# A drain of GpSimd's queue behind the gather of the last slot's rows, in a fused Mamba block and mixture of experts

## The chip, the cores and the metric

The kernel runs on one core of a Trainium2 chip. The time is the device time of one execution, in microseconds (us); of several runs the median is given. A profiled execution also has a span, from its first to its last instruction, and every time inside it is counted from the span's start. Engines: TensorE (PE, with its weight loads apart as PEld), VectorE (DVE), ScalarE (ACT), GpSimd (POOL) and SyncE (SP), which here issues the plain DMAs. A "q" behind a name (POOLq) is the engine's sequencer, which takes the program's instructions in order and runs the ones that need no datapath itself.

## What is computed

Two residual sublayers on x of 8 x 512 tokens with 256 features, each under an adaptive layer norm whose shifts, scales and gates come from a small projection of `c`. The first sublayer is a Mamba-like block (projection, causal convolution, a linear scan, a gate). The second, where the change lies, is a mixture of 8 experts with hidden size 1024, and each token goes to one expert:

```python
logits = x @ wr + br
probs = jax.nn.softmax(logits, axis=-1)
top_p, top_i = jax.lax.top_k(probs, 2)
gate = top_p[:, 0] / (top_p[:, 0] + top_p[:, 1])
top1 = top_i[:, 0]
out = jnp.zeros_like(x)
for e in range(n_experts):
    hmid = jax.nn.gelu(x @ w1[e] + b1[e], approximate=False)
    hout = hmid @ w2[e] + b2[e]
    mask = top1 == e
    out = out + jnp.where(mask[:, None], hout * gate[:, None], 0.0)
```

The reference runs every expert on every token. The kernel runs each expert only on the tokens that chose it.

## The kernel before

*Two stages.* The first runs the Mamba block over the 8 batches, writes each token's row (features, statistics, gate and the modulation vectors, 1028 floats) to the scratch `xp_d` in DRAM, and lists the tokens of each expert in `ids_d`, by 32 indirect DMAs of GpSimd (line 937). The second works through "slots". A pair slot is 256 tokens of one expert (two tiles of 128), a single slot 128.

*A slot's work.* `name_tokens` (line 1023) loads the slot's token numbers, on SP. `fetched` (1150) calls `expert_of` (1035), which loads the expert's weights and biases on SP, and `rows_of` (1055), which gathers the token rows into a tile `xg` by one indirect DMA of GpSimd for each tile of 128. `made` (1283) modulates and transposes them, `layer1` (1083) multiplies by w1 and applies Gelu, and `layer2` (1259) multiplies by w2 into the PSUM tile `py`, finishes the rows on VectorE in the tile `ot`, and scatters them to the output, again by one indirect DMA of GpSimd for each tile. `ot` has two buffers and so has `py`.

*The loop.* `work` (1289) runs over the slots with three slots fetched ahead. There are 20 slots that always run: 16 pairs and 4 singles, so 36 tiles, 36 gathers and 36 scatters. The last slot is a pair; it is fetched in the pass n = 16. Behind the loop stand two branches (`tc.If`, line 1323) for up to three more single slots, which depend on how the tokens fell; with these inputs neither is taken. In a branch's place GpSimd's sequencer then runs an INC_SWDGE_SEM[...]. After that the program closes (line 1379): among others a DRAIN on each engine, and barriers between them.

*What sets the order.* Instructions of the loop are not emitted as written. They are recorded in a `Plan`, with a length each from a table in the code, a due time, and the tiles that they read and write. `order` (191) then simulates all queues greedily: of the instructions whose inputs and buffers are there, the one that can start first goes first, and at equal starts the one that is due first. An indirect DMA is held for 1.3 on GpSimd's queue and lands 9.0 later; what waits for a DMA starts 2.2 after it has landed (`reach`, 277). `plan.call` (121) records any function as an instruction, with a queue, the tiles it reads and writes, and a length. The result is the program order of each engine; on the chip the waits are semaphores.

Of the kernel before, what the change touches and what calls it, by code (L numbers as in the profile page):

```python
# [289 lines left out]
def adaln_mamba_moe_kernel(  # L290
# [15 lines left out]
    nc = tc.nc  # L306
# [29 lines left out]
    plan = Plan(tc)  # L336
    chip, nc = nc, plan
# [93 lines left out]
    with tc.tile_pool(name="wa", bufs=1) as wa, tc.tile_pool(  # L431
# [591 lines left out]
        def name_tokens(i):  # L1023
            jb, at_ = tiles(i), where[i][1]

            def fn():
                o = chip.sync.value_load(at_, min_val=0, max_val=E * TOK)  # L1027
                chip.sync.dma_start(  # L1028
                    out=ids[:, i, 0:jb],
                    in_=ids_d[bass.ds(o, jb * P), :].rearrange("(p j) o -> p (j o)", j=jb),  # L1030
                )

            loads(fn, [ids[:, i, 0:jb]], [at_, *id_views[: FEW * NT]], 0.8)

        def expert_of(i, w1t, w2t, b1t, b2t, behind=()):

            number = where[i][0]

            def fn():
                e = chip.sync.value_load(number, min_val=0, max_val=E - 1)  # L1040
                chip.sync.dma_start(  # L1041
                    out=w1t, in_=w1[bass.ds(e, 1)].rearrange("o (k p) f -> p (o k) f", p=P)
                )
                chip.sync.dma_start(out=b1t, in_=par[:, bass.ds(e * KF, KF)])
                chip.sync.dma_start(
                    out=b2t, in_=b2[bass.ds(e, 1)].rearrange("o d -> (o d)").partition_broadcast(P)
                )
                chip.sync.dma_start(
                    out=w2t, in_=w2[bass.ds(e, 1)].rearrange("o (k p) d -> p (o k) d", p=P)
                )  # L1050

            loads(fn, [w1t, b1t, b2t, w2t], [number, *behind], 2.5)
            return i, w1t, b1t, b2t, w2t

        def rows_of(i, xg, upto):

            for j in range(tiles(i)):
                nc.gpsimd.indirect_dma_start(
                    out=xg[:, j, :], out_offset=None, in_=xp_d[0:upto, :],
                    in_offset=bass.IndirectOffsetOnAxis(ap=ids[:, i, j : j + 1], axis=0),  # L1060
                    bounds_check=upto - 1, oob_is_err=False,
                )
            return xg
# [19 lines left out]
        def layer1(t, hT, gl, ph_tile):  # L1083
            i, w1t, b1t, b2t, w2t, xg = t
            n = tiles(i) * P
            for f in range(KF):
                ph = ph_tile()
                for k in range(KD):
                    nc.tensor.matmul(
                        ph[:, 0:n], lhsT=w1t[:, k, f * P : (f + 1) * P], rhs=hT[:, k, 0:n],  # L1090
                        start=(k == 0), stop=(k == KD - 1),
                    )
                nc.scalar.activation(gl[:, f, 0:n], ph[:, 0:n], AF.Gelu, bias=b1t[:, f : f + 1])
            return gl
# [43 lines left out]
    with tc.tile_pool(name="g", bufs=2) as gp, tc.tile_pool(  # L1138
# [6 lines left out]
        plan = nc = Plan(tc, plan)  # L1145
# [4 lines left out]
        def fetched(i, xg=None):  # L1150
            t = expert_of(
                i, wts.tile([P, KD, FF], FP, name="w1t"), wts.tile([P, KF, D], FP, name="w2t"),
                blk.tile([P, KF], FP, name="b1t"), blk.tile([P, D], FP, name="b2t"),
            )
            if xg is None:

                at = next(turn) % 5
                pool, n = (blk, 3) if at < 3 else (blk2, 2)
                xg = rows_of(
                    i, pool.tile([P, JB, ROW], FP, name="xg", tag=f"xg_{n}", bufs=n),  # L1160
                    FEW * L if i < NEARLY else TOK + BLK,
                )
            return (*t, xg)

        got = [slot0, fetched(1, pre[1])] + [fetched(i) for i in range(2, NEARLY)]
# [90 lines left out]
        slots = list(range(NEARLY)) + [NEARLY + i for i in order]  # L1256
        assert sorted(slots + rest) == list(range(NEARLY + NSLOT))

        def layer2(t, gl):

            i, w1t, b1t, b2t, w2t, xg = t
            mg = xg[:, :, OWN:ROW]
            ot = gp.tile([P, JB, D], FP, name="ot")
            for j in range(tiles(i)):
                py = ps_y.tile([P, D], FP, name="py")
                for f in range(KF):
                    nc.tensor.matmul(
                        py, lhsT=gl[:, f, j * P : (j + 1) * P], rhs=w2t[:, f, :],
                        start=(f == 0), stop=(f == KF - 1),
                    )  # L1270
                nc.vector.tensor_tensor(ot[:, j, :], py, b2t, ALU.add)
                nc.vector.tensor_tensor(ot[:, j, :], ot[:, j, :], mg[:, j, 2 * D : 3 * D], ALU.mult)
                nc.vector.scalar_tensor_tensor(
                    ot[:, j, :], ot[:, j, :], xg[:, j, D + 2 : D + 3], xg[:, j, 0:D],
                    ALU.mult, ALU.add,
                )
                nc.gpsimd.indirect_dma_start(
                    out=outf[i * JB + j],
                    out_offset=bass.IndirectOffsetOnAxis(ap=ids[:, i, j : j + 1], axis=0),
                    in_=ot[:, j, :], in_offset=None, bounds_check=TOK - 1, oob_is_err=False,  # L1280
                )

        def made(t):
            return features(
                t[0], t[-1], gp.tile([P, JB, D], FP, name="hg"),
                gp.tile([P, KD, BLK], FP, name="hT"), ps_r.tile([P, KD, BLK], FP, name="tp"),
            )

        def work(slots, got, begun=None):


            ahead, pending = len(got), None
            hT = None if begun else made(got[0])
            for n in range(len(slots)):
                nc.due = behind + (n + 1) * SLOT
                if n + ahead + 1 < len(slots):
                    name_tokens(slots[n + ahead + 1])
                if n + ahead < len(slots):
                    got.append(fetched(slots[n + ahead]))
                if n == 0 and begun:  # L1300
                    nxt = begun[2]
                else:
                    nxt = made(got[n + 1]) if n + 1 < len(slots) else None
                if n == 0 and begun:
                    layer2(*begun[:2])
                else:
                    gl = layer1(
                        got[n], hT, gp.tile([P, KF, BLK], FP, name="gl"),
                        lambda: ps_h.tile([P, BLK], FP, name="ph"),
                    )  # L1310
                    if pending is not None:
                        layer2(*pending)
                    pending = (got[n], gl)
                hT = nxt
            layer2(*pending)

        name_tokens(slots[NEARLY])
        work(slots, got, (slot0, gl0, hTs[1]))
        plan.emit()
        nc = chip  # L1320
        more = nc.values_load(filled[0:1, 0:1], min_val=0, max_val=NSING)
        for at, part in ((FIRST, rest[:1]), (FIRST + 1, rest[1:])):
            with tc.If(more > at):
                for i in part:
                    name_tokens(i)
                work(part, [fetched(i) for i in part])
# [56 lines left out]
```

## Time and profile before

| | before |
|---|---|
| median of 3 runs | 602.8 us (600.97 to 606.39) |
| the profiled execution | 602.82 us |
| its span | 601.0 us |
| mean granted TensorE clock | 0.968 |
| busy: PE / DVE / ACT / POOL | 563.9 / 351.4 / 210.5 / 209.3 us |
| indirect DMAs of GpSimd: lists / gathers / scatters | 32 / 36 / 36 |
| first start of a gather / last end of a scatter's issue | 284.1 / 589.86 us |

A group's line on the page has the source line, the engine and the operation, what is written and read, and the count; behind the bar the busy time and the mean length of one in ns; behind the second bar the idle time of the engine just before, and what ended most of it. All operations that the plan records have line 154 or 159, since it issues them, so groups are told apart by their tiles. For an indirect DMA the time shown is[...] not that of the transfer. Instructions of a sequencer do not count as busy: they are found by asking for a line's instructions.

### The profile page before, as it was taken

How to read it: one execution, taken by the hardware profiler on the slowest of the kernel's cores; microseconds unless marked ns; L12 is line 12 of the kernel's file. 1: busy time of each engine (PE TensorE's matmuls, PEld its weight loads, DVE VectorE, ACT ScalarE, POOL GpSimd, SP SyncE). 2: the span in 40 equal slices, each digit the busy share in tenths (PEclk: the TensorE clock that was granted, in tenths of full speed). 3: DMA queues.
4: the chain of work that ended last, by engine and by line, in shares of the span. 5: the costliest groups of instructions: out<-in, count | busy, mean ns of one | idle time of the engine just before them, and what ended most of it. 6: DMA issues, size and time to landing. Idle time of an engine off the chain costs nothing. (4 is left out here: it accounts for less than half of the span.)

```text
span 601.0 us, 8691 instructions
## 1 busy us (share of the span) xinstructions
PE 563.9 (94%) x2882; PEld 430.1 (72%) x2882; DVE 351.4 (58%) x1087; ACT 210.5 (35%) x404; POOL 209.3 (35%) x334
## 2 busy tenths in 40 slices
PE   5999999999999999999999938999999999999990
PEld 2454766677675766767678826889888988988980
DVE  4879978987878786784876516325234343532210
ACT  2328544544553634432512210223221422222320
POOL 1513663736254453530424142233223322231110
PEclk9779999999999999999999977999999999999996
DMA  7359999410200001010829996999977977972000
GB/s 276 119 148 196 273 254 238 63 51 14 85 1 18 20 1 37 0 37 1 256 72 254 171 342 225 298 382 331 332 245 237 299 252 244 305 245 71 26 3 16
DMA packets 58703, 96.73 MB, mean 161 GB/s; under 512 B 9852, under 2 KB 41854, under 8 KB 58656
## 3 DMA queue, kind: packets, MB, share of 16 engines
q1 hardware_dynamic: 50720, 72.98, 41.2%
q0 software_dynamic: 7936, 23.17, 11.4%
q8 instruction: 24, 0.39, 0.3%
q14 instruction: 23, 0.19, 0.2%
HBM read 86.42 MB, written 22.81 MB: 182 GB/s over the span
## 5 line engine op out<-in xcount | busy, mean ns | idle before, releaser
L159 ACT ACTIVATE gl<-ph,b1t 128x256 f32<-128x256 f32 (+1 forms) x152 | 68.5, 452 | 186.8 <-PE ph L154 180.7
L154 PE MATMUL py<-w2t,gl 128*128 128x256 f32 x476 | 109.8, 383 | 0.0
L154 PEld LDWEIGHTS py<-w2t,gl 128*128 128x128 f32 x476 | 91.7, 193 | 12.9
L159 POOL DMA_INDIRECT out<-ot,ids x36 | 37.7, 1047 | 159.7 <-DVE ot L159 148.6
L159 DVE SCALAR_TENSOR_TENSOR sv<-u,pt,sv 128x512 f32<-128x512 f32 x96 | 77.2, 809 | 12.7 <-ACT sv L159 12.4
L159 PE MATMUL ph<-hT,w1t 128*128 128x256 f32 (+1 forms) x304 | 84.3, 359 | 0.0
L154 PE MATMUL ph<-hT,w1t 128*128 128x256 f32 (+1 forms) x304 | 84.2, 359 | 0.0
L159 DVE TENSOR_TENSOR ot<-py,b2t 128x256 f32<-128x256 f32 x34 | 14.4, 425 | 109.3 <-PE py L154 105.4
L159 PE MATMUL px<-xnT,wi 128*128 128x512 f32 x128 | 69.6, 626 | 0.0
L154 PE MATMUL px<-xnT,wi 128*128 128x512 f32 x128 | 65.9, 597 | 0.0
L154 PEld LDWEIGHTS ph<-hT,w1t 128*128 128x128 f32 x304 | 55.6, 191 | 6.3
L159 PEld LDWEIGHTS ph<-hT,w1t 128*128 128x128 f32 x304 | 55.0, 191 | 6.2 <-issue 0.4
L159 POOL DMA_INDIRECT xg<-xp_d,ids x36 | 37.8, 1051 | 60.9 <-DMA ids<-ids_d 40.5
L159 POOL DMA_INDIRECT ids_d<-tok,row x32 | 34.8, 1087 | 36.1 <-DVE row L159 13.7
L154 PEld LDWEIGHTS px<-xnT,wi 128*128 128x128 f32 x128 | 24.6, 192 | 31.2 <-issue 31.2
L159 ACT COPY u<-px 128x512 f32<-128x512 f32 x32 | 18.7, 585 | 62.6 <-PE px L154 62.1
L159 DVE COPY hT<-tp 128x512 f32<-128x512 f32 (+1 forms) x20 | 12.7, 634 | 36.3 <-PE tp L154 28.1
L159 PEld LDWEIGHTS px<-xnT,wi 128*128 128x128 f32 x128 | 21.3, 192 | 16.4 <-issue 14.8
L159 POOL TENSOR_TENSOR rs<-ve,nhalf 128x4 f32<-128x4 f32 x16 | 19.5, 1219 | 38.7 <-DVE ve L159 29.0
L159 ACT ACTIVATE tz<-px 128x512 f32<-128x512 f32 x32 | 19.1, 595 | 39.3 <-PE px L154 35.7
L159 DVE TENSOR_TENSOR hg<-hg,xg 128x256 f32<-128x256 f32 x72 | 28.9, 422 | 1.2
L159 DVE TENSOR_TENSOR xr<-po,h 128x256 f32<-128x256 f32 x32 | 13.5, 421 | 25.6 <-PE po L154 25.3
(347 smaller groups left out, 947.2 us busy)
## 6 DMA issues: line engine op xcount, KB each, us to landing
w1t<-in_w SPq DMA_DIRECT2D x19, 1024.0 KB
w2t<-in_w SPq DMA_DIRECT2D x19, 1024.0 KB
xp_d<-modb_d SPq DMA_DIRECT2D x8, 1536.0 KB
xp_d<-xr SPq DMA_DIRECT2D x8, 520.0 KB
xt<-in_x SPq DMA_DIRECT2D x8, 512.0 KB
bc<-mod_d SPq DMA_DIRECT2D x7, 384.0 KB
b2t<-in_b SPq DMA_DIRECT2D x19, 128.0 KB
w<-in_w SPq DMA_DIRECT2D x2, 1024.0 KB
```

The costliest lines, as they stand in the source:

```text
L154: me["calls"].append(lambda: getattr(getattr(self.nc, name), op)(*args, **kw))
L159: calls=[lambda: getattr(getattr(self.nc, name), op)(*args, **kw)],
```

## The change

In `work`, behind the fetch of the last slot, the plan gets one more instruction on GpSimd's queue: `drain()`, which has no operand. For the planner it reads the last slot's tile `xg`, writes nothing, and takes 8.0. It is recorded only while the plan is built, not in the branches behind the loop.

```diff
                 if n + ahead < len(slots):
                     got.append(fetched(slots[n + ahead]))
+                    if nc is plan and n + ahead == len(slots) - 1:
+
+                        plan.call("gpsimd", chip.gpsimd.drain, [], [got[-1][-1]], 8.0)
                 if n == 0 and begun:
                     nxt = begun[2]
```

## The prediction

> **What bounds the kernel now.** I read the page first, then the chain of waits, then the instructions that belong to the program's closing lines, then a table of stretches over the last 16 us, and last GpSimd's instructions in order of time around the place of the edit. The page:
>
> ```profile
> span 601.0 us, 8691 instructions
> ...
> PE   5999999999999999999999938999999999999990
> ...
> L159 POOL DMA_INDIRECT out<-ot,ids x36 | 37.7, 1047 | 159.7 <-DVE ot L159 148.6
> ...
> L159 POOL DMA_INDIRECT xg<-xp_d,ids x36 | 37.8, 1051 | 60.9 <-DMA ids<-ids_d 40.5
> L159 POOL DMA_INDIRECT ids_d<-tok,row x32 | 34.8, 1087 | 36.1 <-DVE row L159 13.7
> ```
>
> TensorE is busy in every slice but the last, so up to about 587 us the time is TensorE's, and GpSimd's waits there (159.7 us before the scatters) cost nothing. GpSimd issues 36 + 36 + 32 = 104 indirect transfers. The last slice of row PE is 0: the end belongs to something else. The chain of waits does not help there: it stops at 589.86 us, with the last scatter, and puts 47.48 us down to a transfer issued at 540.43, which is only the semaphore that a later instruction tested last. What fills the end is seen at line 1379, where the program closes, at line 1323 (the two branches that are not taken) and, for comparison, at line 1371, where it opens. The columns are count, then ns min/median/max, then first and last start in us:
>
> ```profile
> L1379 POOLq DRAIN  x3: 40/107/8560, 591.6 to 600.7; - x3
> L1379 SPq DRAIN  x3: 7/7/7, 592.2 to 600.4; - x3
> L1379 ACTq DRAIN  x2: 8/8/8, 577.6 to 600.4; - x2
> ```
>
> ```profile
> L1323 POOLq INC_SWDGE_SEM  x2: 2242/2244/2245, 585.8 to 589.3; - x2
> ```
>
> ```profile
> L1371 POOLq INC_SWDGE_SEM  x1: 31/31/31, 0.2 to 0.2; - x1
> ...
> L1371 POOLq DRAIN  x1: 179/179/179, 0.4 to 0.4; - x1
> ```
>
> The first of GpSimd's three closing drains, at 591.57, takes 8.56 us; the two behind it 0.107 and 0.040, the one at the start 0.179. Is it a wait for data? The stretches say no (the last two columns are the share of the DMA engines and GB/s):
>
> ```profile
> core 0: us, PE busy (x) PEld busy (x) DVE busy (x) ACT busy (x) POOL busy (x), PEclk, DMA share, GB/s
> ...
> 588.00:590.00 2.00, 0.00 (x0) 0.00 (x0) 0.21 (x1) 0.00 (x0) 0.98 (x1) 0.99 0.05 12
> 590.00:591.00 1.00, 0.00 (x0) 0.00 (x0) 0.00 (x0) 0.00 (x0) 0.00 (x0) 0.50 0.32 111
> 591.00:600.20 9.20, 0.00 (x0) 0.00 (x0) 0.00 (x0) 0.00 (x0) 0.00 (x0) 0.50 0.00 0
> ```
>
> The last scatter's packets move before 591.0; after that no engine computes and no DMA engine moves a byte for 9.2 us. So the drain is work of GpSimd's own that is left from before. A drain with nothing issued before it costs 0.04 to 0.18 us; this one has 104 transfers behind it: (8.56 - 0.11) / 104 = 0.081 us each, if it is a price per transfer. That is my reading, and the forecast hangs on it.
>
> **The change.** It adds one instruction, moves one scatter behind it in GpSimd's order, and removes nothing.
>
> *Where it goes.* The planner holds the drain back until the last slot's rows are there. In the planner's own clock, used here for the order alone, the second gather of the last slot starts at 542.20, so the drain may start at 542.20 + 1.3 + 9.0 + 2.2 = 554.70; GpSimd is free from 552.11; the second scatter of the slot then being finished is ready at 554.73. The drain goes first, by 0.03. GpSimd's stretch in the trace:
>
> ```profile
> 527.30 1.05 POOL L159 DMA_INDIRECT xg<-xp_d,ids  x1 [0.30 <-issue]
> 528.65 1.02 POOL L159 DMA_INDIRECT xg<-xp_d,ids  x1 [0.31 <-issue]
> 536.78 1.03 POOL L159 DMA_INDIRECT out<-ot,ids  x1 [7.10 <-DVE ot L159]
> 540.43 1.01 POOL L159 DMA_INDIRECT out<-ot,ids  x1 [2.62 <-DVE ot L159]
> 551.45 0.98 POOL L159 DMA_INDIRECT out<-ot,ids  x1 [10.01 <-DVE ot L159]
> 554.91 0.98 POOL L159 DMA_INDIRECT out<-ot,ids  x1 [2.48 <-DVE ot L159]
> ```
>
> So it stands between the scatters of 536.78 and 540.43.
>
> *What it costs there.* It starts at 537.81. Of 36 scatters 28 lie before it, so it deals with 32 + 36 + 28 = 96 transfers: 0.11 + 96 x 0.081 = 7.9 us, to 545.7. Queued behind it on GpSimd are the scatter of 540.43 (it goes to about 545.9, 5.5 us late) and the one of 551.45, which finds GpSimd free from 547 and is on time. Who waits for the late scatter? Only the reuse of its `ot` buffer, one of two:
>
> ```profile
> 562.52 0.42 DVE L159 TENSOR_TENSOR ot<-py,b2t 128x256 f32<-128x256 f32 x1 [2.76 <-PE py L154]
> ```
>
> A scatter's packets ended 2.1 us (the one of 536.78) to 3.4 us (540.43) after its start; from 545.9 that is 549.3, 13 us before the write. The last rows' gathers stand ahead of the drain, and SP's queue is not touched. On the planner's clock the late scatter frees its buffer at 575.2 and the first write comes at 578.08, so no other engine's order moves. Cost on the path: 0. Without that cover it would be the 7.9 us in full.
>
> *What it saves.* At the closing drain 8 transfers are left: 0.11 + 8 x 0.081 = 0.76 us in place of 8.56, a gain of 7.8. The closing drain cannot end before the last scatter has landed, though: its packets end at 590.88, and SyncE finds its semaphore set at 591.63.
>
> *The two semaphore increments at line 1323.* They run on GpSimd's sequencer, 2.24 us each. The first ends at 588.01 and the last scatter follows at 588.88, 0.67 after its data (588.21), where the scatters before it follow 0.28 after theirs: 0.39 lost. The second ends at 591.54, and only then does the drain begin. With nothing outstanding the same instruction took 0.031 (line 1371); with 103 and 104 transfers behind it 2.242 and 2.245. So after the change each costs between 0.03 and 2.245. With 7 or 8 outstanding the nearer row is that of none, so I take 0.2. Then the last scatter starts at 588.49, its packets end 2.0 later at 590.5, and it has landed by about 590.9 (between 590.5 and 591.2, from the 0.75 above); the drain ends at 591.0, and the tail of 0.84 (600.13 to 600.97) follows: span 591.9, gain 9.1. With the increments unchanged: 591.57 + 0.76 + 0.84 = 593.2, gain 7.8.
>
> **Two rules of the Trainium skill against it.** The trace has drains of 7 to 17 ns at the close on SyncE, ScalarE, VectorE and TensorE. "VectorE: DVE Perf Modes", section "The DRAIN you can't avoid", calls such drains boilerplate of about 12 ns on all five engines, the same for every kernel; by that there is nothing to win, and the time stays at 602.8. The four engines agree; GpSimd's 8,560 ns does not, and the row decides. "PSUM — Partial Sum Buffer", section "Engine vs sequencer instructions", says that a drain waits until its engine is fully idle. If that were all, the new drain would end at 537.9 and take nothing off the closing one, which would then be a cost that any first late drain pays. But GpSimd's last instruction ended at 589.86, 1.7 us before the closing drain began: idleness alone does not explain 8.56 us. The rule leaves open a price per transfer or a fixed one. No run here shows which.
>
> **The rivals.**
>
> *The price is fixed.* GpSimd's closing drain costs 8.5 us whenever any indirect transfer has gone before it since the last drain, or the new drain deals with none of it. For: only one such drain is in the trace. Against: 0.107 and 0.040 follow at once, so the work can be used up. Then 602.8, because the new drain is covered.
>
> *The price per transfer holds, the increments stay at 2.24.* For: 2.242 and 2.245 differ by less than one part in 104. Against: 0.031 at the start. Then 593.2 + 1.8 = 595.0.
>
> *Slower: the drain holds the scatter too long.* If it takes D us, the late scatter lands at 537.81 + D + 0.2 + 3.4, and the write of 562.52 starts to wait from D = 21. TensorE has the second of two `py` buffers and a layer 1 to do, up to 576.2, so the end moves by D - 34. With the gain of 7.8 it is slower from D = 42, or 0.44 us a transfer, five times the 0.081. At 0.55 a transfer (D = 53) it ends near 613. For it: the drain now runs while the weights' loads keep the DMA engines busy, which the closing one did not. Against: the factor.
>
> **How the numbers follow.** The profiled execution took 602.82 us, 1.8 over its span of 601.0, and is level with the median of the runs, 602.8. Both readings gain: increments shrinking, 591.9 + 1.8 = 593.7, chance 0.48; increments unchanged, 595.0, chance 0.31. Fixed price or no effect, 602.8: 0.14. Slower: 0.07. The likeliest is 593.7. The range runs from 591.8 (the landing at its early end and 1.5 us of scatter between runs, which went from 600.97 to 606.39) to 597.5 (595.0 with the same and a little over), which holds the first two cases, about 0.78, and leaves out the rest. About 1% (6 us) is what can be told from no change here: under 596.8 is faster. From the cases, faster 0.77, same 0.16, slower 0.07.
>
> **What would show it.** Right: a drain of 7 to 9 us on GpSimd from about 538, the scatter behind it near 546, no new wait before the write of 562.5, a first closing drain of 2 us or less, and increments far under 2.24. Wrong: a first closing drain that is still 8 us (fixed price), a new drain of a few tenths of a us (it does nothing), or a write of `ot` that waits for its scatter (held too long).

## The result, and the profile after

| | before | after |
|---|---|---|
| median | 602.7 us (4 runs, 600.97 to 606.39) | 595.14 us (4 runs, 591.9 to 595.28) |
| profiled execution / span | 602.82 / 601.0 us | 595.11 / 593.2 us |
| last scatter but one starts / span ends | 585.04 / 601.0 us | 585.90 / 593.2 us |
| from that start to the end ("the tail") | 15.96 us | 7.30 us |

The ratio is 0.9869, with a 95% interval of 0.983 to 0.9908: 1.3% faster, and at the weak end of the interval 0.9%. Ratios here and below are formed over the runs in the chip's faster state alone, while medians are of all runs, so a ratio is not exactly the quotient of the medians shown. The page of the changed kernel:

```profile
span 593.2 us, 8692 instructions
...
PE   5999999999999999999999875999999999999996
```

The last slice of row PE is 6 where it was 0: the empty end is nearly gone. GpSimd around the new drain, in order of time (start, length, then in brackets the idle time before and what ended it):

```profile
537.64 1.03 POOL L159 DMA_INDIRECT out<-ot,ids  x1 [7.11 <-DVE ot L159]
547.48 1.01 POOL L159 DMA_INDIRECT out<-ot,ids  x1 [8.81 <-issue]
552.32 0.98 POOL L159 DMA_INDIRECT out<-ot,ids  x1 [3.82 <-DVE ot L159]
555.77 0.98 POOL L159 DMA_INDIRECT out<-ot,ids  x1 [2.48 <-DVE ot L159]
```

The second scatter waits 8.81 us for nothing but its turn ("issue"), and the third waits for its data again, so the delay has died out there. The drain itself is an instruction of the sequencer and is found at its own line:

```profile
L286 POOLq DRAIN  x1: 9183/9183/9183, 537.4 to 537.4; - x1
```

Its record begins at 537.41, although in the program it stands behind the scatter of 537.64: the sequencer's record starts before GpSimd is done with what stands ahead (by 2.75 us behind two gathers in a run below). From the end of the scatter's issue (538.67) to the drain's end (537.41 + 9.18 = 546.59) are 7.92 us. That stretch, from the end of the issue ahead to the end of the drain, is what "the drain took" means from here on. The first write of the reused buffer `ot` still waits for its matmul and not for the late scatter:

```profile
563.38 0.42 DVE L159 TENSOR_TENSOR ot<-py,b2t 128x256 f32<-128x256 f32 x1 [2.76 <-PE py L154]
```

At the close (three lines further down in this kernel), count, ns min/median/max, first and last start:

```profile
L1382 SPq EVENT_SEMAPHORE  x14: 17/28/1588, 590.0 to 593.2; - x14
...
L1382 POOLq DRAIN  x3: 46/113/1997, 590.1 to 593.0; - x3
L1382 SPq DRAIN  x3: 7/7/7, 592.4 to 592.7; - x3
```

```profile
L1326 POOLq INC_SWDGE_SEM  x2: 325/325/325, 586.6 to 589.8; - x2
```

The first closing drain fell from 8.56 to 2.00 us, each increment from 2.24 to 0.325. The stretches show what the first closing drain now does:

```profile
core 0: us, PE busy (x) PEld busy (x) DVE busy (x) ACT busy (x) POOL busy (x), PEclk, DMA share, GB/s
...
590.00:591.00 1.00, 0.00 (x0) 0.00 (x0) 0.00 (x0) 0.00 (x0) 0.33 (x1) 0.57 0.16 57
591.00:593.20 2.20, 0.00 (x0) 0.00 (x0) 0.00 (x0) 0.00 (x0) 0.00 (x0) 0.50 0.08 28
```

Before, 9.2 us went by with a DMA share of 0.00. Now the last scatter's packets end at 591.36, within the drain's time (590.12 to 592.12). The price of its 8 transfers alone would have ended it at 590.88: it has become a wait for the landing.

*Which wait ends last at the close.* SyncE runs a row of EVENT_SEMAPHORE instructions, which test one semaphore after the other. The longest of its 14, the 1.588 us from 590.18 to 591.76, ends 0.40 us after the last scatter's packets and is the wait for them. Nine more tests follow about 0.06 us apart, then two drains, the last at 592.41; GpSimd goes on at 592.44, though its own drain ended at 592.12. So GpSimd's drain has 0.3 us to spare, and SyncE's row is what ends last. Before, the same row ran from 591.63 to 592.31 and was covered by the long drain. The runs below agree: where the closing drain is longer (3.33 and 2.67 us) GpSimd goes on 0.04 us after it, and where it is shorter (1.85 to 2.29 us) GpSimd goes on 0.03 us after the second of those SyncE drains.

*An offset that is not the change's.* In the profiled execution everything from about 400 us on runs 0.87 us later than before, up to the tail. The offset arises between 314 and 375 us, where the first stage gives way to the second, and ahead of the new drain. In other executions it is larger and goes both ways (in the experiments below -5.1 to +3.3 us against the kernel before), so spans of single executions are not compared with each other. The tail is: 15.96 - 7.30 = 8.66 us of gain, and 8.66 - 0.87 = 7.8 us is what is left in the span (601.0 - 593.2).

### The profile page after: what moved, and what is told of

It is laid out like the page before. It is cut to its first block, busy times and chain, and to the rows that moved or that the text cites. A ratio compares the mean times of both kernels' runs of the same rounds, so it can differ in the third digit from the quotient of the medians.

```text
span 593.2 us, 8692 instructions
## 1 busy us (share of the span) xinstructions
PE 564.6 (95%) x2882; PEld 430.7 (73%) x2882; DVE 351.0 (59%) x1087; ACT 210.7 (36%) x404; POOL 209.4 (35%) x334
## 3 DMA queue, kind: packets, MB, share of 16 engines
q0 software_dynamic: 7936, 23.17, 11.5%
## 5 line engine op out<-in xcount | busy, mean ns | idle before, releaser
L154 PEld LDWEIGHTS ph<-hT,w1t 128*128 128x128 f32 x304 | 55.6, 191 | 6.3
```

The lines of the kernel that those rows point to most:

```text
L154: me["calls"].append(lambda: getattr(getattr(self.nc, name), op)(*args, **kw))
```

## The experiments

The theory: the drain's time is work for each transfer that GpSimd has issued since its last drain (called its walk below); a transfer is paid for once, at the end or earlier; the increments shrink with it; and in the middle the drain is covered by other work. The rivals: a fixed price, a cover that fails, and no effect of the drain itself. Below, "left" is the number of transfers left for the closing drain, and an offset is how much later than in the kernel before the scatters of a run's second stage start where no drain delays them (with a minus, earlier). Each edit is shown against the kernel that the text ahead of it names; "..." marks lines left out.

**Earlier, so that more is left.** The changed kernel, with the drain behind the tenth slot's fetch instead of the last one's.

```diff
-                    if nc is plan and n + ahead == len(slots) - 1:
+                    if nc is plan and n + ahead == 9:
 
-                        plan.call("gpsimd", chip.gpsimd.drain, [], [got[-1][-1]], 8.0)
+                        plan.call("gpsimd", chip.gpsimd.drain, [], [got[-1][-1]], 5.0)
```

> The drain stands behind the gathers of the tenth slot instead of the last, and nowhere else (planned length 5.0). 61 or 62 indirect transfers lie before it, 42 or 43 behind it. Price per transfer (0.082 us each, and 0.02 us each for a semaphore increment): the new drain lasts about 5.1 us, the first closing drain 0.11 + 42 x 0.082 = 3.6 us, each increment at the branches about 1.0 us, span about 594.7. Fixed price (a drain costs 8 us whatever the number): new drain 8 us, closing drain 2.0 us as in the changed kernel, increments 0.33 us, span about 593.2.

It took 591.27 us (span 589.4), but its offset is -4.65 us. GpSimd's increments and closing drains:

```profile
L1326 POOLq INC_SWDGE_SEM  x2: 962/964/965, 581.1 to 584.2; - x2
```

```profile
L1382 POOLq DRAIN  x3: 46/107/3325, 585.2 to 589.1; - x3
```

With 40 left the closing drain takes 3.325 us, as a price per transfer has it: 0.11 + 40 x 0.0813 = 3.36. A fixed price would leave 8.5 or 2. The tail is 9.0 us. The miss: the new drain itself, with 64 transfers, took 8.5 us in place of 5.3 (taken up at the end of this section).

**Both drains.** The changed kernel, with the drain of the last experiment added.

```diff
                         plan.call("gpsimd", chip.gpsimd.drain, [], [got[-1][-1]], 8.0)
+                    if nc is plan and n + ahead == 9:
+
+                        plan.call("gpsimd", chip.gpsimd.drain, [], [got[-1][-1]], 5.0)
```

> The changed kernel with a second drain behind the gathers of the tenth slot. Price per transfer, each transfer paid once: the early drain about 5.1 us, the later one only for the 34 or 35 transfers between them, 2.9 us instead of 7.9; closing drain 2.0 us, span as the changed kernel (593.2) within 0.5. Fixed price, or a price for all transfers since the start: the later drain again 7.9 us or more.

594.94 us, span 593.1.

```profile
L286 POOLq DRAIN  x2: 4052/7272/10493, 418.7 to 537.2; - x2
```

The later drain now took 2.79 us (538.44 to 541.22) where the change's took 7.92; it has 32 transfers to deal with, and 0.11 + 32 x 0.0813 = 2.71. So what the early one had dealt with was gone: each transfer is paid once. Increments (0.322, 0.325), closing drain (2.06) and tail (7.43) are those of the change. The early one took 8.5 us again.

**More transfers, without rows.** The kernel before, with 24 small plain transfers of GpSimd (16 rows of 4 bytes) that nothing reads, and no drain.

```diff
+        tiny = tab.tile([P, 24], FP, name="tiny")
...
+                    if nc is plan and 4 <= n + ahead < 16:
+                        for k in range(2 * (n + ahead) - 8, 2 * (n + ahead) - 6):
+                            plan.ops[-1]["calls"].append(lambda k=k: chip.gpsimd.dma_start(
+                                out=tiny[0:16, k : k + 1], in_=par[0:16, k : k + 1]
+                            ))
```

> The kernel before, without a drain, and with 24 small direct transfers added to GpSimd's queue (16 rows of 4 bytes each, two behind the gathers of each of 12 slots; what they load is not used). Price per transfer: first closing drain 0.11 + 128 x 0.0813 = 10.5 us, increments 2.7 to 2.8 us. Price per row moved (104 transfers of 128 rows, so the 24 add 3 in 100): closing drain 8.8 us, increments 2.3 us. Fixed price: 8.56 and 2.24 us.

605.38 us, span 603.6, tail 18.9 us. The increments, and then the closing drains:

```profile
L1329 POOLq INC_SWDGE_SEM  x2: 2722/2728/2733, 585.7 to 589.5; - x2
```

```profile
L1385 POOLq DRAIN  x3: 46/103/10523, 592.2 to 603.3; - x3
```

10.523 us against 10.5 expected for 128 transfers: (10.523 - 8.560) / 24 = 0.082 us for each added one. By rows it would have been 8.8. By DMA packets, of which the small transfers have 32 each and the others 76 on average (8704 in all against 7936), it would have been 9.4. The span is about that of before, so the price does not go by time either. It goes by the transfer, whatever its size, and whether it is indirect or not.

**The cover taken away.** The kernel before, with a drain directly ahead of the last scatter.

```diff
+                if nc is plan and i == slots[-1] and j == JB - 1:
+                    plan.ops[-1]["calls"].insert(0, chip.gpsimd.drain)
```

> The kernel before with the drain put directly ahead of the last scatter, where no other engine has work left. If the gain is only that the drain's time is hidden: the new drain lasts about 8.5 us, the last scatter starts about 8 us later, the closing drain shrinks to 2.0 us, and the span stays within 1 us of 601.0. If a drain in the program is cheaper than one at the close: the new drain is well under 8 us and the span nears 593.

598.72 us, span 596.9, with an offset of -3.61 us. Tail: 581.43 to 596.9 = 15.5 us, against 15.96 with no drain added.

```profile
581.43 0.98 POOL L159 DMA_INDIRECT out<-ot,ids  x1 [2.48 <-DVE ot L159]
592.96 0.98 POOL L159 DMA_INDIRECT out<-ot,ids  x1 [10.55 <-DMA out<-ot,ids]
```

```profile
L286 POOLq DRAIN  x1: 9700/9700/9700, 581.2 to 581.2; - x1
```

```profile
L1381 POOLq DRAIN  x3: 46/112/1847, 593.6 to 596.6; - x3
```

The closing drain is down to 1.85 us and the increments to 0.19, but the added drain takes 8.49 us (582.41 to 590.90) on the path, and the last scatter starts 10.55 us after the one before it was issued. The work did not get less: the change's gain is its place.

**The last place with cover, and the change once more.** The kernel before, with a drain behind the scatters of the last pair slot but one, and beside it the changed kernel on the same chip, both over several runs.

```diff
+                if nc is plan and i == slots[-3] and j == JB - 1:
+                    plan.call("gpsimd", chip.gpsimd.drain, [], [outf[i * JB + j]], 1.0)
```

> The kernel before with the drain put later than in the change: behind both scatters of the last pair slot but one, in the longest idle stretch of GpSimd (12.95 us before). 101 transfers lie before it, 3 behind it. Price per transfer: the new drain 8.3 us and still covered, increments at the branches 0.2 to 0.25 us, and a closing drain that ends when the last scatter has landed, so the end is no earlier than in the changed kernel: from the start of the last scatter but one to the end 7.3 us, time equal to the changed kernel within 0.5 us. If each transfer left at the close costs its 0.08 us on top of the landing: 0.4 us less. If the drain is not covered there: the last scatters start later.

> The changed kernel once more, for comparison in the same session: ratio to before about 0.987, closing drain 2.0 us, increments 0.33 us.

| on one chip | median of all runs | ratio to before (95%) | tail of the profiled one |
|---|---|---|---|
| before, 21 runs | 603.02 us | | |
| the change, 6 runs | 598.06 us | 0.9887 (0.983 to 0.9944) | 7.49 us |
| drain later, 16 runs | 594.86 us | 0.9855 (0.9827 to 0.9883) | 7.35 us |

```profile
L286 POOLq DRAIN  x1: 9538/9538/9538, 567.9 to 567.9; - x1
```

```profile
L1381 POOLq DRAIN  x3: 46/112/1937, 589.7 to 592.7; - x3
```

The later drain deals with 101 transfers in 8.32 us (569.14 to 577.47), and the scatter behind it waits 12.95 us for its data as before. With 3 left instead of 8 the closing drain ends 0.57 us after the last packet instead of 0.76, and the tail is the same, since SyncE's row ends last. The intervals overlap: this is not shown to be better than the change. The change's second profile has increments of 0.32 us and a closing drain of 2.11.

**Held too long.** The changed kernel with 37 small operations of GpSimd behind the drain, which write a tile that nothing reads: 40 us more in the place of the drain.

```diff
+        busy = tab.tile([P, NT], FP, name="busy")
...
-                        plan.call("gpsimd", chip.gpsimd.drain, [], [got[-1][-1]], 8.0)
+                        def held():
+                            chip.gpsimd.drain()
+                            for _ in range(37):
+                                chip.gpsimd.tensor_tensor(busy, prio[:, 0:NT], nhalf, ALU.pow)
+
+                        plan.call("gpsimd", held, [], [got[-1][-1]], 8.0)
```

> The changed kernel with 37 small operations added on GpSimd directly behind the drain (1.2 us each, their result is not used), so that the scatter behind it is held for about 53 us in all: the case of the drain that holds the scatter too long. If the reading of the cover is right: VectorE's first write of the slot's `ot` waits for the scatter's landing (about 33 us after its data), TensorE stands still for some 18 us, and the span is 593.2 + 18 = about 611. If the `ot` buffer is not what binds: no wait on VectorE, span about 593 to 600.

612.82 us, span 611.0. GpSimd in order of time, then VectorE, then the longest waits between 540 and 612 us (us in total, times, longest):

```profile
549.11 40.09 POOL L1306 TENSOR_TENSOR busy<-prio,nhalf 128x4 f32<-128x4 f32 x37 [8.02 <-issue]
589.38 1.05 POOL L159 DMA_INDIRECT out<-ot,ids  x1 [0.18 <-issue]
```

```profile
592.66 0.42 DVE L159 TENSOR_TENSOR ot<-py,b2t 128x256 f32<-128x256 f32 x1 [29.62 <-DMA out<-ot,ids]
```

```profile
DVE ot L159 <- DMA out<-ot,ids: 29.6, 1, 29.6
...
PEld py L159 <- DVE ot L159: 13.8, 1, 13.8
PE py L159 <- DVE ot L159: 13.4, 1, 13.4
```

The chain that the prediction named is there link by link: the write of `ot` waits for the late scatter, then TensorE for the second `py` buffer that VectorE cannot empty. From the scatter ahead of the drain to the end it is 540.06 to 611.0 = 70.9 us, against 537.64 to 593.2 = 55.6: 15.4 us longer, where the rule "D - 34" gives 14 for D = 48.1 (541.09 to 589.2). The standstill itself is 13.4 us. Behind it TensorE's granted clock is low for a while (0.57, where the same matmuls ran at 1.00 in the kernel before), and the next 16 matmuls take 5.2 us in place of 3.5:

```profile
593.00:597.00 4.00, 3.86 (x10) 3.18 (x11) 2.24 (x6) 0.00 (x0) 1.94 (x2) 0.57 0.17 58
```

That the span fits the expected 611 is in part luck: the hold was 5 us shorter than planned, and 2.4 us are offset against the changed kernel. The 37 operations change neither the increments (0.32 us) nor the tail (7.3): the price does not count GpSimd's other instructions.

**Where the long early drains come from.** Two of the runs above had shown 8.5 us for 64 transfers. First the changed kernel with the drain directly behind the last slot's gathers, then with two drains in such places; last the kernel before with one drain away from any gather, while the DMA engines are busy.

```diff
-
-                        plan.call("gpsimd", chip.gpsimd.drain, [], [got[-1][-1]], 8.0)
+                        plan.ops[-1]["calls"].append(chip.gpsimd.drain)
```

> The changed kernel with the drain issued directly behind the last slot's two gathers, ahead of the scatter that the planner had put before it. 95 transfers: 0.11 + 95 x 0.081 = 7.8 us from the end of the gathers' issue, or until the gathers have landed, if that is later. The next scatter starts about 1 us late and nobody waits for it: from the start of the last scatter but one to the end 7.3 us, as in the changed kernel. If the place matters: more than 0.5 us away from that.

589.99 us, span 588.0, with an offset of -4.5 us; tail 7.45 us, near the change's.

```profile
L286 POOLq DRAIN  x1: 12653/12653/12653, 522.4 to 522.4; - x1
```

From the end of the gathers' issue the drain took 9.9 us (525.18 to 535.09) for 95 transfers, where the price alone gives 7.8, and the scatter behind it came 3.7 us late instead of 1.

```diff
-                    if nc is plan and n + ahead == len(slots) - 1:
+                    if nc is plan and n + ahead in (9, len(slots) - 1):
-
-                        plan.call("gpsimd", chip.gpsimd.drain, [], [got[-1][-1]], 8.0)
+                        plan.ops[-1]["calls"].append(chip.gpsimd.drain)
```

> The changed kernel with two drains that each stand directly behind a slot's gathers: one behind those of the tenth slot, one behind those of the last slot. The first walks about 61 transfers (0.11 + 61 x 0.0813 = 5.1 us), the second only about 34 (2.9 us). Price per transfer alone: 5.1 and 2.9 us after the end of the issue of the gathers ahead. Theory (a), the walk is slower while the DMA engines are busy: some 1.3 times that, 6.6 and 3.7 us. Theory (b), the drain also waits until the transfers issued ahead of it have landed: both end with the landing of those gathers, 6.5 to 10 us after the end of their issue, the second no sooner than the first although it has half the transfers. Closing drain with about 7 or 8 transfers left in every theory: its walk is short, and it ends some 2 us after it began, with the landing of the last scatter.

589.19 us, span 587.3, tail 7.34 us. The two drains:

```profile
L286 POOLq DRAIN  x2: 10187/11004/11822, 400.8 to 521.8; - x2
```

From the end of the gathers' issue the first took 9.1 us (403.50 to 412.60) for 61 transfers and the second 7.4 us (524.59 to 532.03) for 34, where the price alone gives 5.1 and 2.9. A walk that is 1.3 times slower would have made the second 3.7. That the second would end no sooner than the first, as expected for a wait for the landing alone, did not come true either.

```diff
+                if nc is plan and i == slots[8] and j == 0:
+                    plan.ops[-1]["calls"].append(chip.gpsimd.drain)
```

> The kernel before with a drain directly behind a scatter in the middle of the last stages, about 452 us, where no gather stands just ahead but the DMA engines are about 0.65 busy; about 72 transfers since the last drain. Price per transfer alone, or with (b) a wait for the landing of one scatter (2.4 us, shorter than the walk): 0.11 + 72 x 0.0813 = 6.0 us after the end of that scatter's issue. Theory (a), a slower walk while the DMA engines are busy: 7 us or more. Closing drain with about 32 left: 2.7 us; the two increments about 0.18 + 31 x 0.02 = 0.8 us each.

```profile
L286 POOLq DRAIN  x1: 7225/7225/7225, 447.9 to 447.9; - x1
```

```profile
452.00:455.00 3.00, 3.00 (x16) 2.59 (x16) 0.00 (x0) 1.49 (x4) 0.00 (x0) 1.00 0.83 286
```

591.74 us, span 589.9. From the end of the scatter's issue (449.13) it took 5.96 us for 72 transfers, with 0.83 of the DMA engines' time taken in its second half (the last column but one above): the price alone (6.0), so DMA engines this busy did not slow the walk. Closing drain (2.67) and increments (0.805) with 32 left are as expected, and the tail is 8.2 us. So the long ones wait for the gathers just ahead of them. Not the whole of it, though: the gathers' last packets ended at 409.58 and 530.26, 3.0 and 1.8 us ahead of the drains' ends. The seven drains that ran into a landing (61, 64, 64, 95, 34, and 8 twice) ended 3.0, 3.1, 3.1, 4.3, 1.8, 0.76 and 0.77 us after the last packet, which fits 0.44 + 0.040 us for each transfer, half the price. Closing drains that this fit did not use agree with it: with 9, 3 and 1 left they ended 0.82, 0.57 and 0.48 us after the last packet, for 0.80, 0.56 and 0.48. It looks as if half of the walk could start only after the landing; what happens in the drain is not shown, and no run was made to test it.

## Why the prediction was right

Point by point; the forecast was faster, near 593.7 us, and 595.14 lies in its range (591.8 to 597.5).

*The price per transfer: right.* 0.081 us was read from one drain. Closing drains with 128, 104, 40 and 32 transfers took 10.52, 8.56, 3.33 and 2.67 us, which is 0.11 + 0.0813 for each within 0.05. The fixed price is out.

*The place and its cost there: right.* The drain took 7.92 us for 7.9, between the two scatters named. The scatter behind it came 7.05 us later than before (547.48 against 540.43), 6.2 without the offset, for 5.5: between drain and scatter lie 0.9 us with four small sequencer instructions, where 0.2 was taken. No wait came of it.

*The increments: right in kind, with a size guessed.* 0.325 us for 0.2. The last scatter starts 0.28 us after its data (589.35, with a gain of 0.40 against the offset, for 0.39). The rival "increments unchanged" is out, although its 595.0 lies next to the median of 595.14: it would have had 2.24 us at that line. That its number fits is chance, made by the offset and the mis-sized term that follow.

*The close: a term mis-sized.* Landing is as worked out: 2.41 us after the last scatter's start for 2.4. Then the prediction let GpSimd's drain end 0.1 us after the landing and counted a tail of 0.84, 0.9 together. Measured from the landing that SyncE saw (591.76) to the end (593.2) are 1.4 us. The drain ends 0.35 us after it, and even that is not what counts: SyncE's nine tests behind the one for the last scatter and its drains take 0.65 us to 592.41. That row stood in the trace of before, under the 8.56 us; the prediction asked what is late next on GpSimd alone.

*The sum.* 591.9 forecast for the span; plus 0.87 for the offset of the earlier stages and 0.5 for SyncE's row gives 593.3, and 593.2 was measured. The former is no step of the change and lies within what runs of one kernel differ by.

*The slower rival: its mechanism right, its condition not met.* With D raised to 48 us the wait was where it said, and TensorE stood still for 13.4 us; the change has 8. Its own figures make the rule D - 34.8 (576.2 less 541.4), which gives 13.3. The lower clock behind the standstill, some 1.7 us more, it did not have. What was argued for it, that busy DMA engines might stretch the drain, fell: a drain took the price alone, 5.96 us, with the engines at 0.83 in its second half. A gather just ahead does stretch it, to 9.9 us at most here, far from 42.

*The two rules.* That closing drains are small boilerplate holds here for four engines and not for GpSimd. The section of the Trainium skill that the prediction named for it, "The DRAIN you can't avoid" of "VectorE: DVE Perf Modes", speaks of drains from the preamble and postamble, while those at line 1379 carry a line of the program: it may not have been meant for them. That a drain waits for an idle engine is not enough: the walk is on top, and so is the landing of what was issued just ahead. What the drain does during its walk no trace shows; that is open.

## What to carry to other kernels

A long drain at the end is not yet a wait: look whether any packet moves under it, count what its engine issued since its last drain, and divide. If it is work per transfer, it can be moved into an idle stretch of that engine, away from a gather just issued and with slack for what is queued behind it; what is left at the end is the landing of the last transfer. And before counting a gain at the close, look for the row of waits on another engine that the long one covered.

## What the runs showed of the hardware

- GpSimd's DRAIN costs about 0.11 us plus 0.0813 us for each DMA that GpSimd issued since its last drain, of 128 indirect rows or of 16 plain ones alike, and it did not end before those had landed (it ended 1.8 to 4.3 us after the last packet behind a gather with 34 to 95 transfers to walk, and 0.48 to 0.82 at the close with 1 to 9).
- INC_SWDGE_SEM costs by the same count, plain transfers included. The first of the two took 0.183 us with none left behind a drain, 0.325 with 7, 0.805 with 31, 0.96 with 39, 2.24 with 103 and 2.73 with 127, or about 0.183 + 0.020 each; the second, a scatter later, differed from it by at most 0.011. At the program's start it is 0.031 us.
- A transfer that is long done still counts until a drain has dealt with it: in the kernel before, the earliest of the 104 was issued at 96 us, some 495 us before the closing drain.
